# The relation-count product of a two-layer graph kernel: one float32 product against bfloat16 products on a table split in three

## Chip, cores, metric

One core of a Trainium2 chip. The metric is the device time of the kernel in microseconds, the median of repeated executions; all executions quoted here are fast (TensorE's granted clock 0.99 of full speed).

## The reference

128 graphs of 64 nodes with 768 features pass through two pre-norm layers. Only layer 0 matters here. `adj` holds 0 and 1, and serves both as the matrix and as the relation ids.

```python
h = jnp.maximum(_layernorm(x), 0.0)
ctx = jnp.matmul(adj, hs @ Wadj.T + badj) / deg_c[..., None]
ctx = ctx + jnp.matmul(radj, hs @ Wrev.T + brev) / rdeg_c[..., None]
ctx = ctx + hs @ Wself.T + bself
agg = jnp.einsum('bij,bijr->bir', adj, E[rels])
rel = agg @ Wr.T + br * deg[..., None]
ragg = jnp.einsum('bij,bijr->bir', radj, E[rr])       # rr: reversed ids + 40
rel = rel + ragg @ Wrr.T + brr * rdeg[..., None]
x = x + ctx + rel
```

## The kernel before

Two graphs make a tile of 128 rows, 64 tiles in all. The relation term is written as (count of each id in a row) times (id x E[id] W^T): 78 counts and 5 bias factors, one more product into the sums of layer 0. The program is unrolled, and the compiler of the kernel language orders each engine's instructions itself, by priority and by what it believes to be ready; every engine then runs its list strictly in that order. The stages are emitted as b(t), e(t-2), c(t), a(t+1), f(t-2), d(t-1).

```python
psb = tile_pool(name="psb", bufs=2, space=PSUM)       # products, two banks each
pss = tile_pool(name="pss", bufs=4, space=PSUM)       # transposes, one bank each
...
def stage_a(t):                                       # VectorE: counts of rows and columns
    H0[t] = norm_relu(X[t], "h0", 1)
    for d in range(2):
        eq = work.tile([P, NV, N], BF16, name="eq", bufs=1)
        nc.vector.tensor_tensor(eq, AB[c][...], vals, op=OP.is_equal)
        nc.vector.tensor_reduce(CNT[c][:, k, d*NV:(d+1)*NV], eq, AX.X, OP.add)

def stage_b(t):
    pt = pss.tile([P, 3, P], F32, name="ps")
    for d in range(2):
        nc.tensor.transpose(pt[:, d, :], ABD[c][:, k, d, :], ident)      # L252
    nc.tensor.transpose(pt[:NROW, 2, :], CNT[c][:, k, :], ident)         # L253
    r = R[t] = work.tile([P, 2, P], F32, name="r")
    nc.scalar.copy(r, pt[:, 0:2, :])                                     # L255
    CT_T[t] = work.tile([NROW, P], F32, name="cntT")
    nc.scalar.copy(CT_T[t], pt[:NROW, 2, :])                             # L257
    for kb in range(KB):
        ps = pss.tile([P, 3, P], F32, name="ps")
        nc.tensor.transpose(ps[:, 2, :], hb_, ident)                     # L262
        nc.tensor.matmul(ps[:, 0:2, :], hb_, r, start=True, stop=True)   # L263
        nc.scalar.copy(s1[:, kb], ps)

def stage_c(t):
    ... 36 float32 products of 384 columns                               # L275
    for hf in range(2):
        nc.tensor.matmul(pc[:, hf, :HALF], CT_T[t],
                         tab[:, hf*HALF:(hf+1)*HALF], start=False, stop=True)   # L280
    nc.vector.tensor_add(xv, pc[:, :, :HALF], xv)                        # L283, the residual add
    H1[t] = norm_relu(X[t], "h1", 3)
```

## Time and profile before

| | before |
|---|---|
| median time (three executions) | 3142.4 us (3140.8 to 3143.3) |
| TensorE busy, share of the chain | 98%, 95% |
| one tile in the steady state (L340 of one tile to the next, 2906.20 to 3050.08 us over three) | 47.96 us |
| first stage of tile 0 / of tile 1 starts | 37.0 us / 73.4 us |
| VectorE waits for TensorE ahead of tile 0's residual add | 18.5 us |

The chain of waits is nearly all TensorE, so the time is read as: start, plus 64 periods of TensorE's list, plus an end. The prediction shows the lines for the period.

### The profile page before, as it was taken

Reading aid. Unit: us, or ns where it says so; the run is one execution under the profiler, and the core shown is the slowest. Engines: PE = TensorE matmul, PEld = TensorE weight load, DVE = VectorE, ACT = ScalarE, POOL = GpSimd, SP = SyncE. Lnnn points to the kernel's source line nnn. Section 1 sums busy time; section 2 is a strip of 40 time slices with the busy share of each in tenths; the row PEclk is TensorE's granted clock in tenths of the full one; section 3 lists DMA queues with packets and bytes.
Section 4 is the critical chain, followed back from the end, with each engine's and each line's share of the span. In section 5 each row is a group of like instructions: output and inputs, shape, how many; then the busy total and the mean of one; then the engine's idle time right before and its main releaser. Section 6 shows DMA issues by size and latency. Waiting matters only on the chain.

```text
span 3139.9 us, 27406 instructions
## 1 busy us (share of the span) xinstructions
PE 3065.2 (98%) x10952; PEld 1908.4 (61%) x10952; DVE 1721.6 (55%) x2250; ACT 632.0 (20%) x1217; POOL 560.0 (18%) x556
## 2 busy tenths in 40 slices
PE   5999999999999999999999999999999999999997
PEld 3666666666666666666666666666666666666664
DVE  6356545565445565455654455654556544556344
ACT  1121121121121211211211212212112112122121
POOL 1112122121121121221211211212212112112121
PEclk8999999999999999999999999999999999999998
DMA  5000000000000000000000000000000000000000
GB/s 202 1 22 22 12 22 20 12 22 12 22 21 12 22 22 12 22 21 12 22 12 22 21 12 22 22 12 22 20 12 22 12 22 20 12 22 22 11 16 16
DMA packets 41065, 70.18 MB, mean 22 GB/s; under 512 B 19941, under 2 KB 20069, under 8 KB 40938
## 3 DMA queue, kind: packets, MB, share of 16 engines
q1 hardware_dynamic: 35840, 54.54, 5.4%
q10 hardware_dynamic: 5098, 13.89, 1.1%
q8 instruction: 87, 1.43, 0.2%
q14 instruction: 40, 0.33, 0.0%
HBM read 43.24 MB, written 25.17 MB: 22 GB/s over the span
## 4 chain that ended last, share of the span: by engine, by line
PE 95%; ACT 3%; DMA 1%; issue 1%; DVE 0%; ACTq 0%; POOL 0%; SPq 0%
PE pb L275 47%; PE pb L302 32%; PE ps L263 6%; PE pb L368 3%; PE pb L280 3%; PE ps L340 1%; ACT h1t L296 1%; ACT pT L364 1%; PE ps L363 1%; ACT r L255 1%; PE ps L262 1%; DMA wh<-in_w_cat_dram 0%; DMA xt<-in_x_dram 0%; PE ps L295 0%; ACTq L134 0%
## 5 line engine op out<-in xcount | busy, mean ns | idle before, releaser
L275 PE MATMUL pb<-w,s 128*128 128x384 f32 x4608 | 1496.6, 486 | 0.0
L275 PEld LDWEIGHTS pb<-w,s 128*128 128x128 f32 x4608 | 875.8, 190 | 609.9
L302 PE MATMUL pb<-wh,h1t 128*128 128x384 f32 x1536 | 512.5, 490 | 5.4 <-ACT h1t L296 0.6
L302 PE MATMUL pb<-wg,h1t 128*128 128x384 f32 x1536 | 505.8, 486 | 0.0
L283 DVE TENSOR_TENSOR xt<-pb,xt 128x768 f32<-128x768 f32 x64 | 61.3, 957 | 782.7 <-PE pb L280 782.6
L302 PEld LDWEIGHTS pb<-wg,h1t 128*128 128x128 f32 x1536 | 291.9, 190 | 203.4
L302 PEld LDWEIGHTS pb<-wh,h1t 128*128 128x128 f32 x1536 | 286.7, 190 | 207.0 <-ACT h1t L296 20.6
L243 DVE TENSOR_REDUCE cnt<-eq 128x39 f32<-128x2496 bf16 x128 | 352.4, 2753 | 3.2
L364 ACT COPY pT<-ps 128x384 f32<-128x384 f32 x128 | 55.2, 482 | 1294.6 <-PE ps L363 1294.5
L311 POOL MEMSET hs<- 128x6 f32 x64 | 7.3, 114 | 1377.5 <-PE pb L368 1377.5
L263 PE MATMUL ps<-r,h 128*128 128x256 f32 x768 | 209.5, 395 | 8.3
L241 DVE TENSOR_TENSOR eq<-ab,vals 128x2496 bf16<-128x2496 bf16 x128 | 186.6, 1458 | 3.6
L319 POOL TENSOR_TENSOR pr<-th,wsd 128x768 f32<-128x768 f32 x64 | 116.0, 1812 | 351.9 <-ACT th L309 351.9
L264 ACT COPY s<-ps 128x384 f32<-128x384 f32 x384 | 159.1, 497 | 46.1 <-PE ps L263 45.9
L342 DVE TENSOR_TENSOR a<-ps,sd 128x384 f32<-128x384 f32 x64 | 35.7, 557 | 213.6 <-PE ps L340 213.6
L263 PEld LDWEIGHTS ps<-r,h 128*128 128x128 f32 x768 | 128.0, 194 | 40.6 <-ACT r L255 23.0
L325 DVE TENSOR_TENSOR tg<-pb,hbb 128x768 f32<-128x768 f32 x64 | 61.3, 957 | 134.8 <-PE pb L302 134.8
L345 POOL MEMSET lm<- 128x384 f32 x64 | 26.7, 417 | 608.2 <-ACT pbd L353 608.2
L193 DVE BATCH_NORM_STATS2 st<-xt 128x6 f32<-128x384 f32 x256 | 127.2, 538 | 5.0 <-DMA xt<-in_x_dram 2.8
L199 POOL TENSOR_TENSOR rs<-ve,mhalf 128x1 f32<-128x1 f32 x128 | 107.7, 851 | 103.0 <-DVE ve L197 102.8
L377 DVE TENSOR_SCALAR e<-f 128x768 f32<-128x768 f32 x64 | 120.5, 1882 | 2.2
L202 ACT ACTIVATE h<-h,rs 128x768 f32<-128x768 f32 x128 | 113.3, 931 | 33.0 <-POOL rs L199 33.0
(70 smaller groups left out, 2300.2 us busy)
## 6 DMA issues: line engine op xcount, KB each, us to landing
xt<-in_x_dram SPq DMA_DIRECT2D x64, 384.0 KB, 3.5
out_dram<-f SPq DMA_DIRECT2D x64, 384.0 KB, 2.6
w<-in_wself_t_dram ACTq DMA_DIRECT2D x3, 768.0 KB, 8.2
w<-in_wadj_t_dram ACTq DMA_DIRECT2D x3, 768.0 KB, 11.2
w<-in_wrev_t_dram ACTq DMA_DIRECT2D x3, 768.0 KB, 13.8
wh<-in_w_cat_dram ACTq DMA_DIRECT2D x3, 768.0 KB, 15.0
wg<-in_hw_t_dram ACTq DMA_DIRECT2D x3, 768.0 KB, 15.4
ai<-in_adj_dram SPq DMA_DIRECT2D x32, 64.0 KB, 2.0
```

The costliest lines, as they stand in the source:

```text
L193: nc.vector.bn_stats(st[:, i, :], src[:, i * HALF : (i + 1) * HALF])
L199: nc.gpsimd.tensor_tensor(rs, ve, mhalf, op=OP.pow)
L202: nc.scalar.activation(h, h, AF.Copy, scale=rs)
L241: nc.vector.tensor_tensor(eq, AB[c][:, k, d, None, :].to_broadcast([P, NV, N]), vals, op=OP.is_equal)
L243: nc.vector.tensor_reduce(CNT[c][:, k, d * NV : (d + 1) * NV], eq, AX.X, OP.add)
L263: nc.tensor.matmul(ps[:, 0:2, :], hb_, r, start=True, stop=True)
L264: nc.scalar.copy(s1[:, kb], ps)
L275: nc.tensor.matmul(pc[:, hf, :HALF], S1T[t][:, kb, s, :], ws[s][:, kb, hf * HALF : (hf + 1) * HALF], start=(n == 0), stop=False)
L280: nc.tensor.matmul(pc[:, hf, :HALF], CT_T[t], tab[:, hf * HALF : (hf + 1) * HALF], start=False, stop=True)
L302: nc.tensor.matmul(p[:, hf, :HALF], h1t[:, kb, :], w[:, kb, hf * HALF : (hf + 1) * HALF], start=(kb == 0), stop=(kb == KB - 1))
L319: nc.gpsimd.tensor_mul(to, th, wsd[:, s, :])
L377: nc.vector.tensor_scalar(e, f, 0.0, None, op0=OP.min)
```

## The change

The counts are whole numbers up to 64, exact in bfloat16. The float32 table is split into three bfloat16 parts, whose sum is meant to be the table, and the parts are stacked along the contraction, so that one pass with float32 accumulation should give the float32 result. The counts have then to be repeated three times. 81 rows (the five bias rows are folded into three) times three are 243, more than 128: two parts of 126 and 117. The intent is to trade the four passes of a float32 product for two products of one pass each, 645 ns for 2 x 163 ns.

```diff
-    NROW = NCNT + 5
+    NROW = NCNT + 3
+    PARTS = ((0, P // 3), (P // 3, NROW))
...
-    tab = const.tile([NROW, D], F32, name="tab")
+    tabs = [const.tile([3 * (b - a), D], BF16, name=f"tab{a}") for a, b in PARTS]
...  # table: both parts, each row three times, by float32 products; then on VectorE
+        for i in range(3):
+            nc.vector.tensor_copy(q[:m], v[:m])
+            nc.vector.tensor_sub(v[:m], v[:m], q[:m])
+            nc.vector.scalar_tensor_tensor(u[:m], q[:m], part[:m, i : i + 1], u[:m],
+                                           op0=OP.mult, op1=OP.add)
+        nc.vector.tensor_copy(tab, u[:m])
...
-        cnt = CNT[c] = work.tile([P, CT, NROW], F32, name="cnt")
+        cnt = CNT[c] = work.tile([P, CT, NROW], BF16, name="cnt")
...
-        nc.tensor.transpose(pt[:NROW, 2, :], CNT[c][:, k, :], ident)
+        pn = pss.tile([P, 2, P], BF16, name="ps")
+        cn = CT_T[t] = work.tile([P, 2, P], BF16, name="cntT")
+        c3 = work.tile([P, NROW, 3], BF16, name="c3")
+        nc.gpsimd.tensor_copy(c3, CNT[c][:, k, :, None].to_broadcast([P, NROW, 3]))
+        for i, (a, b) in enumerate(PARTS):
+            nc.tensor.transpose(pn[: 3 * (b - a), i, :],
+                                c3[:, a:b, :].rearrange("p v c -> p (v c)"), identb)
+            nc.scalar.copy(cn[: 3 * (b - a), i, :], pn[: 3 * (b - a), i, :])
         r = R[t] = work.tile([P, 2, P], F32, name="r")
         nc.scalar.copy(r, pt[:, 0:2, :])
-        CT_T[t] = work.tile([NROW, P], F32, name="cntT")
-        nc.scalar.copy(CT_T[t], pt[:NROW, 2, :])
...
-            nc.tensor.matmul(pc[:, hf, :HALF], CT_T[t], tab[:, hf * HALF : (hf + 1) * HALF],
-                             start=False, stop=True)
+            for i, (a, b) in enumerate(PARTS):
+                nc.tensor.matmul(pc[:, hf, :HALF], CT_T[t][: 3 * (b - a), i, :],
+                                 tabs[i][:, hf * HALF : (hf + 1) * HALF],
+                                 start=False, stop=(i == 1))
```

More of the change, by code (lines that the diff above doesn't have):

```diff
@@ L74 @@
     NCNT = 2 * NV
-    NROW = NCNT + 5
+    NROW = NCNT + 3
+    PARTS = ((0, P // 3), (P // 3, NROW))
     W = DO + 1
-    assert GT == 2 and N == 64 and DO == P and H == KB and NROW <= P and NT % CT == 0
+    assert GT == 2 and N == 64 and DO == P and H == KB and 3 * (NROW - P // 3) <= P and NT % CT == 0
     xf = x.rearrange("g n d -> (g n) d")
@@ L129 @@
     nc.scalar.dma_start(wrt[:, 1, :], wrr_t)
+    bia = work.tile([5, D], F32, name="bia", tag="pr", bufs=1)
     for i, v in enumerate((br, brr, badj, brev, bself)):
-        nc.scalar.dma_start(tab[NCNT + i : NCNT + i + 1, :], row(v, 1))
+        nc.scalar.dma_start(bia[i : i + 1, :], row(v, 1))
     for w, src in ((ws[2], wself_t), (ws[0], wadj_t), (ws[1], wrev_t), (wh, w_cat), (wg, hw_t)):
@@ L145 @@
     make_identity(nc, ident)
+    identb = const.tile([P, P], BF16, name="identb")
+    nc.vector.tensor_copy(identb, ident)
     blk = const.tile([P, P], F32, name="blk")
@@ L173 @@
                    allow_small_or_imprecise_dtypes=True)
-    es = const.tile([P, 2, NCNT], F32, name="es")
+    es = const.tile([P, 2, NROW], F32, name="es")
     nc.vector.memset(es, 0.0)
@@ L178 @@
                              et[:, d * NB + 1 : (d + 1) * NB], ids)
-    pt = psb.tile([P, 2, 512], F32, name="pb")
-    for hf in range(2):
-        for d in range(2):
-            nc.tensor.matmul(pt[:NCNT, hf, :HALF], es[:, d, :],
-                             wrt[:, d, hf * HALF : (hf + 1) * HALF],
-                             start=(d == 0), stop=(d == 1))
-    nc.vector.tensor_copy(tab[:NCNT, :].rearrange("p (a b) -> p a b", a=2),
-                          pt[:NCNT, :, :HALF])
+    eb = const.tile([5, NROW], F32, name="eb")
@@ new lines @@
+    nc.gpsimd.memset(eb, 0.0)
+    nc.gpsimd.iota(eb[0:1, 0:NV], pattern=[[1, NV]], base=1, channel_multiplier=0,
+                   allow_small_or_imprecise_dtypes=True)
+    ebr = const.tile([1, NROW], F32, name="ebr")
+    nc.gpsimd.memset(ebr, 0.0)
+    nc.gpsimd.iota(ebr[0:1, NV:NCNT], pattern=[[1, NV]], base=1, channel_multiplier=0,
+                   allow_small_or_imprecise_dtypes=True)
+    nc.sync.dma_start(eb[1:2, :], ebr)
+    nc.sync.dma_start(eb[2:5, NCNT:NROW], ident[0:3, 0:3])
@@ new lines @@
+    part = const.tile([P, 3], F32, name="part")
+    for i in range(3):
+        nc.vector.tensor_reduce(
+            part[:, i : i + 1], ident[:, i:P:3],
+            AX.X, OP.add)
+    for (a, b), tab in zip(PARTS, tabs):
+        m = 3 * (b - a)
+        lhs = work.tile([P, 3, P], F32, name="lhs", tag="a", bufs=1)
+        for d in range(2):
+            nc.vector.tensor_copy(lhs[:, d, :m].rearrange("p (v c) -> p v c", c=3),
+                                  es[:, d, a:b, None].to_broadcast([P, b - a, 3]))
+        nc.vector.tensor_copy(lhs[:5, 2, :m].rearrange("p (v c) -> p v c", c=3),
+                              eb[:, a:b, None].to_broadcast([5, b - a, 3]))
+        pt = psb.tile([P, 2, 512], F32, name="pb")
+        for hf in range(2):
+            s = slice(hf * HALF, (hf + 1) * HALF)
+            for d in range(2):
+                nc.tensor.matmul(pt[:m, hf, :HALF], lhs[:, d, :m], wrt[:, d, s],
+                                 start=(d == 0), stop=False)
+            nc.tensor.matmul(pt[:m, hf, :HALF], lhs[:5, 2, :m], bia[:, s],
+                             start=False, stop=True)
+        v = work.tile([P, D], F32, name="tv", tag="e", bufs=1)
+        u = work.tile([P, D], F32, name="tu", tag="th", bufs=1)
+        q = work.tile([P, D], BF16, name="tq", tag="lm", bufs=1)
+        nc.vector.tensor_copy(v[:m].rearrange("p (a b) -> p a b", a=2), pt[:m, :, :HALF])
+        nc.gpsimd.memset(u, 0.0)
+        for i in range(3):
+            nc.vector.tensor_copy(q[:m], v[:m])
[3 more added lines that the diff above has]
+        nc.vector.tensor_copy(tab, u[:m])
@@ L215, in prep_adj @@
         nc.gpsimd.tensor_copy(AB[c], af)
-        cnt = CNT[c] = work.tile([P, CT, NROW], F32, name="cnt")
-        nc.vector.tensor_reduce(cnt[:, :, NCNT : NCNT + 2], af, AX.X, OP.add)
+        cnt = CNT[c] = work.tile([P, CT, NROW], BF16, name="cnt")
+        dg0 = small.tile([P, CT, 2], F32, name="dg0")
+        nc.vector.tensor_reduce(dg0, af, AX.X, OP.add)
         dc = small.tile([P, CT, 2], F32, name="dc")
-        nc.vector.tensor_scalar(dc, cnt[:, :, NCNT : NCNT + 2], 1.0, None, op0=OP.max)
+        nc.vector.tensor_scalar(dc, dg0, 1.0, None, op0=OP.max)
         rc = small.tile([P, CT, 2], F32, name="rc")
         nc.vector.reciprocal(rc, dc)
-        nc.vector.tensor_mul(cnt[:, :, NCNT + 2 : NCNT + 4], cnt[:, :, NCNT : NCNT + 2], rc)
-        nc.vector.memset(cnt[:, :, NCNT + 4 : NCNT + 5], 1.0)
+        nc.vector.tensor_scalar(cnt[:, :, NCNT : NCNT + 2], dg0, 1.0, None, op0=OP.min)
+        nc.vector.memset(cnt[:, :, NCNT + 2 : NCNT + 3], 1.0)
         ABD[c] = abds[c % 2]
@@ L242, in stage_a @@
                 eq, AB[c][:, k, d, None, :].to_broadcast([P, NV, N]), vals, op=OP.is_equal)
-            nc.vector.tensor_reduce(CNT[c][:, k, d * NV : (d + 1) * NV], eq, AX.X, OP.add)
+            with nc.allow_low_precision(reason="whole numbers up to 64"):
+                nc.vector.tensor_reduce(CNT[c][:, k, d * NV : (d + 1) * NV], eq, AX.X, OP.add)
     def stage_b(t):
```

## The prediction

> **What bounds the kernel now.** I read the page first: the busy shares, then the chain that ended last.
>
> ```profile
> span 3139.9 us, 27406 instructions
> PE 3065.2 (98%) x10952; PEld 1908.4 (61%) x10952; DVE 1721.6 (55%) x2250; ACT 632.0 (20%) x1217; POOL 560.0 (18%) x556
> ...
> PE 95%; ACT 3%; DMA 1%; issue 1%; DVE 0%; ACTq 0%; POOL 0%; SPq 0%
> ```
>
> TensorE is both 98% busy and 95% of the chain, so time that is taken off TensorE's stream is time taken off the span, and work on the other engines counts only where TensorE waits for it. The share of the touched product is in the groups by shape:
>
> ```profile
> L275 PE MATMUL pb<-w,s 128*128 128x384 f32 x4608 | 1496.6, 486 | 0.0
> L280 PE MATMUL pb<-tab,cntT 83*128 83x384 f32 x256 | 93.1, 485 | 0.0
> L253 PE MATMUL ps<-ident,cnt 128*83 128x128 f32 x64 | 17.7, 276 | 5.4 <-DVE cnt L243 5.4
> L257 ACT COPY cntT<-ps 83x128 f32<-83x128 f32 x64 | 16.9, 264 | 0.0
> L215 POOL CAST ab<-af 128x256 bf16<-128x256 f32 x32 | 12.7, 396 | 30.0 <-DVE af L213 30.0
> ```
>
> L280 is the count product: 256 records for 64 tiles x 2 halves, so one float32 matmul is two records. The mean of 485 ns is not its price, because the recorded windows overlap (4608 x 486 ns would be 2239 us where the union is 1497). For the price I read the chain in order of time through one tile of the steady state; it gives start-to-start times.
>
> ```profile
> 1564.07 23.22 PE pb L275 x72
> 1587.29 1.29 PE pb L280 x4
> ...
> 1591.88 15.75 PE pb L302 x48
> 1607.63 0.12 PE ps L253
> 1607.75 0.02 issue
> 1607.77 0.38 ACT r L255
> 1608.15 0.04 issue
> 1608.20 1.56 PE ps L263 x6
> ```
>
> 23.22 us / 72 = 322.5 ns per record, so 645 ns per float32 product of 384 columns, and 1.29 us per tile for L280's two products. Over 64 tiles that is 82.6 us, 2.6% of the span: the most that this part could give back. The last five lines show a second thing: after the gate's product TensorE transposes the counts (L253), ScalarE then copies r, and only then can L263 begin. The timeline of TensorE one tile earlier says how much of this is idle:
>
> ```profile
> 1559.50 0.27 PE L253 MATMUL ps<-ident,cnt 128*83 128x128 f32 x1
> 1559.61 0.49 PE L262 MATMUL ps<-ident,h 128*128 128x128 f32 x3
> 1560.24 1.56 PE L263 MATMUL ps<-r,h 128*128 128x256 f32 x6
> ...
> 1591.42 0.38 PE L252 MATMUL ps<-ident,abd 128*128 128x128 f32 x2
> 1591.88 1.56 PE L302 MATMUL pb<-wh,h1t 128*128 128x384 f32 x4
> ```
>
> A float32 transpose starts every 0.11 us here (1559.50 to 1559.61), so three L262 end their slots at 1559.94, and L263 starts at 1560.24: 0.30 us idle per tile. The matrices that r comes from (L252) were transposed early, in the hole ahead of L302; r is late only because its PSUM tile also takes the count transpose. The period is 48.0 us; adding up the slots (72, 4 and 48 records at 0.3225 us, 22 transposes at 0.11, 12 L263 at 0.216, 12 L368 at 0.11, L340 0.645) gives 46.9 us, so all idling is only some 1.1 us per tile.
>
> **What the Trainium skill says.** "Perfetto Trace Analysis", section Tensor Engine Instruction: the profiler's start of a matmul is real, its end is computed. The trace agrees (486 ns windows every 322.5 ns), so I use starts only. "FP8 and Floating Point Precision", section TensorE Precision Notes: true float32 takes four passes through the array. "TensorE: Matmul & The Clock Gate", section Back-to-back issue gap: N / 2.4 + 2.5 ns at full clock. Four passes of 384 columns at 2.4 GHz are 640 ns; the trace has 645 in two records, so it agrees with both. No instruction of this trace is a bfloat16 matmul, so the price of the new product is an estimate from that page: 384 / 2.4 + 2.5 = 162.5 ns, and 55.8 ns for a transpose with 128 columns. "PSUM — Partial Sum Buffer", section on bank collisions: two engines must not touch one bank and quadrant at once, so accesses are to be ordered by bank, not by address. The kernel before never reads one part of a transposed tile before writing the next, so its trace cannot show the effect; the changed one does exactly that.
>
> **The change, part by part.**
>
> *Removed.* Four L280 records per tile (1.29 us), one float32 count transpose (0.11 us), one ScalarE copy of 83x128 (0.26 us, not on the path), and the tie of r to the count transpose (up to 0.30 us).
>
> *Added on TensorE.* Stacking three parts makes 243 rows, more than 128, hence two parts of 126 and 117 rows. That is 2 parts x 2 halves = 4 bfloat16 products of one pass each: 4 x 162.5 = 0.65 us. The threefold contraction costs two instructions for one, not three times. Their weight loads are at most 0.14 us (the shortest float32 load recorded) and hide behind 0.16 us of matmul. Two bfloat16 transposes: 2 x 0.056 = 0.11 us. Net on TensorE's slots: 1.29 + 0.11 - 0.65 - 0.11 = 0.64 us per tile, 41 us over 64 tiles.
>
> *Moved.* r now has a PSUM tile of its own, complete with L252. Those transposes run some 15 us before the stage that uses r, and ScalarE (20% busy) can copy it meanwhile. I expect most of the 0.30 us idle to go: 0.3 x 64 = 19 us.
>
> *Added elsewhere.* GpSimd writes every count three times: 243 bfloat16 elements, near the 256-element cast of 0.40 us, so 64 x 0.4 = 26 us on an engine at 18%. The counts are made by VectorE well ahead (TensorE waited for them twice, both at the start), so this copy should be early too. ScalarE gets two copies of 128 columns for one, +0.26 us per tile. The minimum in place of the product of degrees costs VectorE nothing new.
>
> *Added wait.* Both count transposes write one PSUM bank, and ScalarE copies the first part between them: the second must wait for transpose latency plus copy, 0.27 + 0.26 + handoffs = about 0.6 us. TensorE has three L262 (0.33 us) and L263 pairs (0.43 us each) to put in between, if the instruction order does so. I charge 0.1 us per tile, 6 us.
>
> *Start.* The split table takes VectorE about 2 parts x 11 passes over 768 columns at 0.6 to 0.96 us, some 20 us, and TensorE 24 float32 records instead of 8. The first stage now begins at 36.97 us, held by the queue of DMA issues on ScalarE (until 34.6 us), and the table is read only at 66 us; VectorE fills this time with counts of tiles that are not urgent. Most of it is hidden; I charge 3 us because the order of the first counts and copies may slip.
>
> Sum: 41 + 19 - 6 - 3 = 51 us, or 3142 - 51 = 3091 us, 1.6% faster.
>
> **The rivals.**
>
> *The handoff between the transposes replaces r's wait.* For it: the write-read-write of one bank, and ScalarE having the gate's tanh (0.85 us) in the same stretch, in strict order. Against it: other work lies ready for TensorE. If the whole 0.6 us shows each tile, 38 us are lost: 41 + 19 - 38 - 3 = 19 us gained, 3123 us.
>
> *The gap fillers go further.* With counts ready far ahead, the transposes can slide into the holes before L368 and L302 (about 0.24 us idle each), so they cost nothing, and r's wait goes altogether: (0.645 + 0.30 + 0.11 + 0.1) x 64 = 74 us, 3068 us. For it: L252 sits in such a hole already. Against it: that hole is 0.24 us and L253 was not put there before.
>
> *Only the passes count.* r is copied late for some other reason, as ScalarE's order puts it behind the count copies: 41 - 6 - 3 = 32 us, 3110 us.
>
> *Slower.* The GpSimd copy lands on the path (it queues behind the two 1.81 us products with the tanh), or the table's set-up delays the first stage by 20 us. Either costs up to 60 us; GpSimd's idle stretch of 20 us in every period speaks against the first, the DMA issues until 34.6 us against the second.
>
> **Range and chances.** The 41 us rest on pass counts that the trace confirms; the order of instructions decides the rest, some 20 us either way. I centre between the sum and the second rival's ceiling at 3090 us and hold 3067 to 3115 eight times in ten. Two per cent is 62.8 us, 0.98 us per tile: it needs the idling to go as well as the passes, 22%. Slower by 2% needs a new stall of 1.6 us per tile: 2%.
>
> **What would show it.** In the profile after: four records of L280's successor in 0.65 us of the chain (1.2 or more would say that bfloat16 does not save the passes); no ScalarE copy of r in the chain between L302 and L263; a period near 47.15 us; second count transposes after a ScalarE wait, with TensorE idle below 0.1 us; GpSimd at about 19%; the first product of layer 0 still near 43 us. A first stage beyond 45 us, or GpSimd in the chain, would make the prediction wrong.

## More of the kernel before

CNT, the buffer of the counts, holds a chunk of two tiles and exists twice.

VectorE's timeline around the first residual add and TensorE's at the second tile (start, duration, engine, line, operation; in brackets the idle time before it and what ended it):

```profile
47.38 1.46 DVE L241 TENSOR_TENSOR eq<-ab,vals 128x2496 bf16<-128x2496 bf16 x1
67.36 0.96 DVE L283 TENSOR_TENSOR xt<-pb,xt 128x768 f32<-128x768 f32 x1 [18.52 <-PE pb L280]
```

```profile
73.40 0.48 PE L262 MATMUL ps<-ident,h 128*128 128x128 f32 x1 [5.75 <-ACT h L202]
```

VectorE has 18.5 us of slack there; the second tile's first stage needs a normalisation that stands behind this add in VectorE's list.

## The result, and the profile after

The changed kernel takes 3094.7 us (3092.9 to 3095.7) beside 3142.1 us of the kernel before (four executions): 47.4 us less, ratio 0.985, 95% interval 0.9836 to 0.9864. The gain is clear of the noise, but at the 2% line the verdict is "same". A ratio here is the mean time of one kernel's fast runs over that of the other's fast runs of the same rounds, so it is not quite the ratio of the medians that are quoted.

The line numbers shift: L241 and L243 (the comparison and the reduction that make the counts) are L286 and L289 now, L252 is L298, L253 is L304, L255 is L308, L262/L263 are L313/L314, L275 is L326, L280 is L332, L283 is L336, L302 (heads and gate) is L355, and L340 (the logits' product) is L393. The page of the changed kernel shows the same bound:

```profile
span 3092.7 us, 27801 instructions
PE 3023.1 (98%) x11032; PEld 1886.3 (61%) x11032; DVE 1736.7 (56%) x2281; ACT 643.6 (21%) x1281; POOL 589.8 (19%) x626
```

The chain in order of time, one tile of the steady state (start, duration, what):

```profile
1575.31 15.75 PE pb L355 x48
1591.05 0.06 PE ps L304
1591.11 0.12 PE ps L313
1591.22 0.43 PE ps L314 x2
1591.66 0.06 PE ps L304
...
1594.44 0.65 PE ps L393 x2
1595.08 23.22 PE pb L326 x72
1618.30 0.66 PE pb L332 x4
```

Three things are to be seen. The count products take 0.66 us where they took 1.29. ScalarE's copy of r is gone from between the gate's product and L314: r was copied at 1575.52 us, 15 us early. And the second count transpose stands behind one L313 and one L314, so that ScalarE's copy between the two transposes costs TensorE nothing. From the end of L355 to the start of the logits' product (L393) 3.39 us pass; in the kernel before it was 3.76 us (1607.63 to 1611.39). The period is 46.945 us (L393 at 2909.18 and 3003.07, two tiles), 1.015 us less than before. From the second tile's first stage to the end of the program the profiled execution takes 3003.0 us (3092.7 less 89.7) where it took 3066.5 us (3139.9 less 73.4): 63.5 us less, which is 1.015 us for some 62.5 tiles. That is 16 us more than the whole gain, so 16 us were lost before that, at the start. VectorE's timeline around the first residual add, and TensorE's at the second tile, in the changed kernel:

```profile
66.17 1.46 DVE L286 TENSOR_TENSOR eq<-ab,vals 128x2496 bf16<-128x2496 bf16 x1
67.67 2.75 DVE L289 TENSOR_REDUCE cnt<-eq 128x39 bf16<-128x2496 bf16 x1
...
80.51 2.75 DVE L289 TENSOR_REDUCE cnt<-eq 128x39 bf16<-128x2496 bf16 x1
83.18 0.95 DVE L336 TENSOR_TENSOR xt<-pb,xt 128x768 f32<-128x768 f32 x1
```

```profile
66.59 0.82 PE L332 MATMUL pb<-tab,cntT 126*128 126x384 bf16 x4
...
89.66 0.47 PE L313 MATMUL ps<-ident,h 128*128 128x128 f32 x1 [21.18 <-ACT h L246]
```

TensorE finishes the first tile's products at about 67.4 us, as before, but VectorE comes to the add only at 83.2 us, with no idle before it: it is busy with counts of tiles that nobody needs yet. The second tile starts at 89.7 us instead of 73.4: 16.3 us later. VectorE's list ahead of this add grew by two things: by the table (2 x 11 passes and the small copies, some 16 us) and by counts (from 8 to 12 reductions and from 9 to 12 comparisons, 15.6 us). The theory that I tested: GpSimd's threefold copy reads the counts early and so frees their buffer early, which lets the list's maker put the next chunk's counts into VectorE's hole ahead of the add. (The expectations below price them at 17 us, four pairs of 4.2 us; one of the four comparisons stood there before the change too.) The account closes: in the kernel before, VectorE's list ahead of the add ended at 48.84 us (47.38 + 1.46), now it ends at 83.18 us. These 34.3 us are 15.6 us of counts, 2.4 us more waiting of VectorE, and some 16 us of table; less the hole of 18.5 us they leave 15.8 us, by which the add is late (83.18 against 67.36 us). By these sizes either load alone would fit; e1 shows it for the table.

### The profile page after: what moved, and what is told of

Read it like the earlier page. It is cut to its first block, busy times and chain, and to the rows that moved or that the text cites. A ratio compares the mean times of both kernels' runs of the same rounds, so it can differ in the third digit from the quotient of the medians.

```text
span 3092.7 us, 27801 instructions
## 1 busy us (share of the span) xinstructions
PE 3023.1 (98%) x11032; PEld 1886.3 (61%) x11032; DVE 1736.7 (56%) x2281; ACT 643.6 (21%) x1281; POOL 589.8 (19%) x626
## 4 chain that ended last, share of the span: by engine, by line
PE 94%; DVE 2%; ACT 2%; issue 1%; DMA 0%; POOL 0%; ACTq 0%; SPq 0%; DVEq 0%; POOLq 0%
PE pb L326 47%; PE pb L355 33%; PE ps L314 5%; PE pb L421 3%; PE ps L313 1%; PE pb L332 1%; PE ps L393 1%; ACT h1t L349 1%; ACT pT L417 1%; DVE cnt L289 1%; PE ps L416 1%; DVE eq L286 0%; PE ps L348 0%; PE pb L216 0%; PE ps L304 0%
## 5 line engine op out<-in xcount | busy, mean ns | idle before, releaser
L326 PE MATMUL pb<-w,s 128*128 128x384 f32 x4608 | 1496.6, 486 | 0.0
L326 PEld LDWEIGHTS pb<-w,s 128*128 128x128 f32 x4608 | 877.2, 190 | 608.4
L355 PE MATMUL pb<-wh,h1t 128*128 128x384 f32 x1536 | 512.5, 491 | 5.3 <-ACT h1t L349 0.6
L355 PE MATMUL pb<-wg,h1t 128*128 128x384 f32 x1536 | 505.9, 486 | 0.0
L336 DVE TENSOR_TENSOR xt<-pb,xt 128x768 f32<-128x768 f32 x64 | 61.3, 958 | 743.4 <-PE pb L332 743.4
L355 PEld LDWEIGHTS pb<-wg,h1t 128*128 128x128 f32 x1536 | 292.4, 190 | 202.9
L355 PEld LDWEIGHTS pb<-wh,h1t 128*128 128x128 f32 x1536 | 287.1, 190 | 206.6 <-ACT h1t L349 20.6
L289 DVE TENSOR_REDUCE cnt<-eq 128x39 bf16<-128x2496 bf16 x128 | 352.3, 2752 | 3.1
L314 PE MATMUL ps<-r,h 128*128 128x256 f32 x768 | 219.8, 386 | 0.0
L286 DVE TENSOR_TENSOR eq<-ab,vals 128x2496 bf16<-128x2496 bf16 x128 | 186.7, 1459 | 3.4
L313 PE MATMUL ps<-ident,h 128*128 128x128 f32 x384 | 107.1, 279 | 25.8 <-ACT h L246 25.8
L314 PEld LDWEIGHTS ps<-r,h 128*128 128x128 f32 x768 | 119.2, 196 | 18.1 <-issue 1.4
L306 ACT COPY cntT<-ps 126x128 bf16<-126x128 bf16 (+1 forms) x128 | 34.3, 268 | 429.7 <-PE ps L304 429.7
L243 POOL TENSOR_TENSOR rs<-ve,mhalf 128x1 f32<-128x1 f32 x128 | 107.8, 852 | 76.9 <-DVE ve L241 76.7
```

The source lines that it names most:

```text
L243: nc.gpsimd.tensor_tensor(rs, ve, mhalf, op=OP.pow)
L286: nc.vector.tensor_tensor(eq, AB[c][:, k, d, None, :].to_broadcast([P, NV, N]), vals, op=OP.is_equal)
L289: nc.vector.tensor_reduce(CNT[c][:, k, d * NV : (d + 1) * NV], eq, AX.X, OP.add)
L326: nc.tensor.matmul(pc[:, hf, :HALF], S1T[t][:, kb, s, :], ws[s][:, kb, hf * HALF : (hf + 1) * HALF], start=(n == 0), stop=False)
L355: nc.tensor.matmul(p[:, hf, :HALF], h1t[:, kb, :], w[:, kb, hf * HALF : (hf + 1) * HALF], start=(kb == 0), stop=(kb == KB - 1))
```

## The experiments

"Correct" below means that the output passed the check. The kernel before took 3141.3 us beside e1 to e4 and 3142.3 us beside e5 to e8. Unless the text says otherwise the edit is on the changed kernel.

### e1: hold the counts until TensorE has read them

```diff
-        cnt = CNT[c] = work.tile([P, CT, NROW], BF16, name="cnt")
+        cnt = CNT[c] = work.tile([P, CT, NROW, 3], BF16, name="cnt")
...  # counts, minima and the one are written to [..., 0]
-        c3 = work.tile([P, NROW, 3], BF16, name="c3")
-        nc.gpsimd.tensor_copy(c3, CNT[c][:, k, :, None].to_broadcast([P, NROW, 3]))
+        c3 = CNT[c][:, k]
+        nc.gpsimd.tensor_copy(c3[:, :, 1:3], c3[:, :, 0:1].to_broadcast([P, NROW, 2]))
```

> The changed kernel, but the threefold copies of the counts lie in the counts' own buffer, so that the buffer comes free only when TensorE has transposed them, as in the kernel before. Theory (two loads meet in VectorE's order before the first layer-0 residual add: the table's 19 us and the counts of tiles that the early copy lets in, 17 us; the slack is 18.5 us): the add of tile 0 starts at about 67.3 us instead of 83.2, the second tile's first stage near 73 us instead of 89.7, period unchanged at 46.95 us, time 3095 - 16 = 3079 us (3077 to 3082). Rival (the table alone delays the start): 3095 us within 2. Rival (the early copy is needed in the steady state): period above 46.95 us and a time above 3082 us.

Correct, 3078.4 us (3077.1 to 3078.6), ratio 0.9799 (0.9784 to 0.9814). VectorE's and TensorE's timelines of e1:

```profile
67.36 0.96 DVE L336 TENSOR_TENSOR xt<-pb,xt 128x768 f32<-128x768 f32 x1 [2.26 <-PE pb L332]
```

```profile
73.40 0.48 PE L313 MATMUL ps<-ident,h 128*128 128x128 f32 x1 [5.01 <-ACT h L246]
```

The add waits for TensorE again, the second tile starts at 73.40 us, exactly as in the kernel before, and the period stays 46.95 us. The 16.3 us come back as 16.3 us of time. The table's work is still all there, so the table alone does not delay the start; it leaves 2.26 us of the slack. This version beats both kernels; against the kernel before the interval reaches over the 2% line, so that verdict is unclear.

### e5: the table's split cut to one round

```diff
         for i in range(3):
+            if i > 0:
+                continue
             nc.vector.tensor_copy(q[:m], v[:m])
```

> The changed kernel with the table's split stopped after its first round: the two lower parts of the table stay zero, so the product has bfloat16's precision only; VectorE loses 12 passes over 768 columns, some 9.3 us in the changed kernel's trace, and nothing else; all twelve counts still stand ahead of the residual add in VectorE's order. Theory (the start's delay is the length of VectorE's queue beyond the slack, whatever it is made of): the add of tile 0 at 83.2 - 9.3 = 73.9 us, the second tile's first stage near 80.4 us, time 3094.7 - 9.3 = 3085.4 us (3084 to 3087). Rival (only the early counts matter, the table hides): 3094.7 us within 2; also if VectorE's copies wait for something else, such as TensorE's table products.

Correct, 3087.3 us (3086.3 to 3087.7), ratio 0.9825, 0.3 us above the expected range and far from the rival. The add (L338 here) starts at 74.47 us, still without a wait, and the second tile's first stage at 80.95 us, 8.7 us earlier than in the changed kernel, where 9.3 were expected; some of the removed time turned into waits of VectorE for the table's products. The median fell by 7.4 us, the profiled span by 8.2. VectorE's add in e5:

```profile
74.47 0.95 DVE L338 TENSOR_TENSOR xt<-pb,xt 128x768 f32<-128x768 f32 x1
```

So the length of VectorE's list counts: with the counts in place, less table brings the add forward nearly one to one. With e1 this shows that each of the two loads adds to the delay, and that the table needs the counts to do harm. The reverse, the counts without any table, was not run. An estimate: the ten passes of table that are left in e5 take 7.2 us in its trace, and the add is still 7.1 us late, so the counts alone would just about fit. A by-product: the run still passed as correct, so this check cannot tell the exact split from its first part.

### e2: the table's split on GpSimd

```diff
-            nc.vector.tensor_copy(q[:m], v[:m])
-            nc.vector.tensor_sub(v[:m], v[:m], q[:m])
-            nc.vector.scalar_tensor_tensor(u[:m], q[:m], part[:m, i : i + 1], u[:m],
-                                           op0=OP.mult, op1=OP.add)
-        nc.vector.tensor_copy(tab, u[:m])
+            nc.gpsimd.tensor_copy(q[:m], v[:m])
+            nc.gpsimd.tensor_sub(v[:m], v[:m], q[:m])
+            nc.gpsimd.tensor_scalar(q[:m], q[:m], part[:m, i : i + 1], None, op0=OP.mult)
+            nc.gpsimd.tensor_add(u[:m], u[:m], q[:m])
+        nc.gpsimd.tensor_copy(tab, u[:m])
```

> The changed kernel with the splitting of the table (14 passes over the 768 columns, 15.5 us of VectorE) on GpSimd; nothing else moves in the orders of the engines. Theory (both loads together exceed the slack of 18.5 us): VectorE's queue ahead of the residual add ends near 83.2 - 15.5 = 67.7 us, the second tile's first stage starts near 74 us, time about 3079 us (3077 to 3083). Rival (counts alone delay the start, the table is hidden): 3095 us within 2. If GpSimd's slower passes hold up the table itself beyond 66 us, the count product of tile 0 waits and the time lies between 3083 and 3095.

Correct, 3090.6 us (3089.6 to 3091.8), a miss: 4 us gained where 16 were expected. (The time lies in the last band of the expectation, but not for the reason given there: the table came late, and yet it is VectorE that holds the add. The edit also moves 20 passes and not 14.) VectorE's timeline of e2, while GpSimd works on the table:

```profile
54.79 2.83 DVE L286 TENSOR_TENSOR eq<-ab,vals 128x2496 bf16<-128x2496 bf16 x1
57.65 2.75 DVE L289 TENSOR_REDUCE cnt<-eq 128x39 bf16<-128x2496 bf16 x1
60.44 2.28 DVE L286 TENSOR_TENSOR eq<-ab,vals 128x2496 bf16<-128x2496 bf16 x1
...
78.70 0.95 DVE L336 TENSOR_TENSOR xt<-pb,xt 128x768 f32<-128x768 f32 x1
```

The comparisons take up to 2.83 us instead of 1.46 us (3.2 us more in all), while the reductions between them keep 2.75 us. The Trainium skill ("Advanced Engine Details and Errata", section GPSIMD Details) says that GpSimd and VectorE share a read and a write interface and that VectorE instructions with two SBUF inputs are among those that conflict. The trace agrees: the comparisons read two tiles in SBUF, the reductions one. VectorE also waits 6.5 us for GpSimd, since the second part's copy out of PSUM reuses a buffer. The add comes at 78.7 us. The work was moved, but a good part of its cost stayed with VectorE. The second part of the table came at 70.1 us, 3.8 us late for TensorE. As a test of the two loads e2 says little; e5 does it cleanly.

### e3: the kernel before, with the counts' transpose in a tile of its own

```diff
-        nc.tensor.transpose(pt[:NROW, 2, :], CNT[c][:, k, :], ident)
+        pn = pss.tile([P, P], F32, name="ps")
+        nc.tensor.transpose(pn[:NROW, :], CNT[c][:, k, :], ident)
...
-        nc.scalar.copy(CT_T[t], pt[:NROW, 2, :])
+        nc.scalar.copy(CT_T[t], pn[:NROW, :])
```

> The kernel before, float32 product and all, with only the transposed counts moved to a PSUM tile of their own, so that ScalarE can copy r early. Theory (r's wait is 0.30 to 0.37 us of every tile and belongs to the shared tile alone): period 47.96 - 0.3 to 0.37 = 47.6 to 47.66 us, no ScalarE copy of r in the chain, time 3142 - 19 to 24 = 3118 to 3123 us. Rival (the wait went because of the bfloat16 transposes and their order): 3142 us within 3. The start may also move by some us, since the order of the first copies changes.

Correct, 3117.9 us (3116.5 to 3118.8), ratio 0.9925 (0.991 to 0.994): 23.3 us from one PSUM tile, without any bfloat16. The chain of e3:

```profile
1626.24 15.75 PE pb L303 x48
1641.99 0.11 PE ps L254
1642.10 0.11 PE ps L263
1642.21 0.43 PE ps L264 x2
...
1645.36 0.65 PE ps L341 x2
```

ScalarE's copy of r is out of the chain. From L303's end to the logits' product 3.37 us pass, against 3.76: 0.39 us. The period is 47.57 us (L341 at 2929.77 and 2977.34), 0.39 us below 47.96. This is more than the 0.30 us that I had read off the timeline as idle: with r early, each L263/L264 pair follows its transpose at once, and the later small stalls of that stage go as well.

### e6: r tied to the counts again, in the changed kernel

```diff
-        pn = pss.tile([P, 2, P], BF16, name="ps")
+        pn = pt[:, 2, :].bitcast(BF16).rearrange("p (a b) -> p a b", a=2)
```

> The changed kernel with the bfloat16 count transposes written into the last third of r's own PSUM tile, as the kernel before had it; same products. Theory (what e3 gave is taken back, and the write-read-write of one bank now shows as well): the copy of r is back in the chain between the gate's product and the first (A h) product; at least 0.37 us per tile, and by the chain transpose 0.27 + copy 0.26 + transpose 0.27 + copies of counts and r 0.27 + 0.37 less the three transposes in between 0.33 us up to 1.0 us per tile: period 47.3 to 47.95 us, time 3118 to 3159 us. Rival (with bfloat16 transposes the tie costs nothing): 3095 us within 3.

Correct, 3159.7 us (3158.9 to 3160.3), ratio 1.0056: slower than the kernel before (the late start is in it too), and 0.7 us beyond the upper end of what I expected. The chain of e6:

```profile
1624.05 0.06 PE ps L304
1624.11 0.33 PE ps L313 x3
...
1624.46 0.23 PE ps L304
...
1624.71 0.27 ACT cntT L306
1624.98 0.28 ACT r L308
...
1625.31 1.56 PE ps L314 x6
```

The period is 48.01 us (2924.98 to 2972.99), 1.07 us above the changed kernel's. All links of the expected path are there: three transposes fill 0.33 us, then the second count transpose, its copy, r's copy, L314. The rival of the prediction, "the handoff between the transposes replaces r's wait", is thus real; it fails to appear in the changed kernel because r has its own bank, the one line in which e6 differs. The tie would have cost more than the bfloat16 products save.

### e4: the kernel before without its count products

```diff
-                                     start=(n == 0), stop=False)
+                                     start=(n == 0), stop=(n == 3 * KB - 1))
...
-        for hf in range(2):
-            nc.tensor.matmul(pc[:, hf, :HALF], CT_T[t], tab[...], start=False, stop=True)
```

> The kernel before without the two count products of each tile; wrong on purpose, it measures what the product cost. Theory (its whole start-to-start time of 1.29 us lies on the path): period 46.67 us, time 3142 - 82.6 = 3059 us (3056 to 3063). Rival (part of it hides waits of other engines that would show without it, such as the exponentials' transposes behind it): above 3065 us.

3058.5 us (3057.6 to 3061.0): 82.7 us less, against 82.6 expected. Its output is wrong, which doesn't matter for the time. The period is 46.67 us. The float32 product cost its start-to-start time to within the noise; nothing was hidden beside it.

### e7: each bfloat16 product twice

```diff
+                for j in range(2):
-                nc.tensor.matmul(..., start=False, stop=(i == 1))
+                    nc.tensor.matmul(..., start=False, stop=(i == 1 and j == 1))
```

> The changed kernel with each of the four bfloat16 count products issued twice (wrong on purpose: the relation term counts double); orders otherwise equal. Theory (a bfloat16 product of 384 columns costs 0.163 us of path, its weight load hidden): 8 records in 1.3 us, period 46.95 + 0.65 = 47.6 us, time 3094.7 + 0.65 x 64 = 3136 us (3134 to 3139). Rival (loads of weights show when products repeat, or part of the cost hides): outside this by more than 5 us.

3134.3 us (3134.1 to 3135.2): 39.6 us more than the changed kernel. Its output is wrong, which doesn't matter for the time. The chain has

```profile
1590.46 1.31 PE pb L333 x8
```

in place of 0.66 us for four, and the period is 47.59 us, 0.65 us up: 0.163 us per product. The missing 2 us lie partly at the start, where the second tile began at 88.6 us instead of 89.7.

### e8: e1 with the weights issued by SyncE

```diff
-            nc.scalar.dma_start(w[:, k : k + 2, :], ...)
+            nc.sync.dma_start(w[:, k : k + 2, :], ...)
...  # likewise the rows bb, hbb, wsd; the two small loads into eb go to ScalarE
```

> The kernel of e1 with the 15 weight loads and the four small rows issued from SyncE's queue in place of ScalarE's, so that ScalarE is free for the first normalisation at about 12 us and not at 35 us. Not a test of the change but a try at the rest of the start. Expected: the first stage begins before 20 us instead of 37.6; the first product then runs as the weights land, and ends near 50 us instead of 66.5, period unchanged 46.95 us; time 3078.4 - 10 to 17 = 3061 to 3068 us. Rival (the start is bound by the weights' 35 us of transfer or by the second activations' chain anyway): 3078 us within 3. If the later loads of x, queued behind the weights, come late, it is slower than e1.

Correct, 3070.8 us (3070.3 to 3072.2), ratio 0.9774 (0.9759 to 0.9789): 7.6 us better than e1 and beyond 2% against the kernel before, but a miss: 10 to 17 us were expected, and the first stage begins at 23.3 us, not before 20. The chain at the start:

```profile
29.81 1.48 PE pb L216 x4
...
33.35 23.22 PE pb L326 x72
56.57 0.67 PE pb L332 x4
57.27 0.96 DVE xt L336
58.23 2.66 DVE cnt L289
```

The first tile's products begin at 33.35 instead of 43.3 us. They are now held by the float32 products of the table (L216), which stand between the transposes in TensorE's list, and the second tile by a count reduction (2.66 us) behind the residual add. So about 10 us are gained and 2.7 given back. This is beside the change; it shows that the start still has a few us in it.

## Why the prediction was right

The predicted 3090 us and the measured 3094.7 us agree, and the steady state changed as the prediction said: four records in 0.66 us of the chain, no copy of r in it, GpSimd at 19%. But the terms of the sum did not all come out. The steady state gave some 10 us more than the sum has, and the start cost 13 us more; that these two errors cancelled is luck.

| step of the prediction | predicted | measured |
|---|---|---|
| passes and transposes, 0.64 us per tile | -41 us | -40 us (1.29 to 0.66 us per tile, e4 and e7) |
| r's idle, 0.30 us per tile | -19 us | -24 us (0.37 to 0.39 us per tile, e3) |
| the transposes' handoff, 0.1 us per tile | +6 us | 0 (no idle in the chain; 1.07 us per tile when r is tied, e6) |
| the start | +3 us | +16.3 us (73.4 to 89.7 us; e1 takes it away) |
| sum | -51 us | -48 us (measured time: -47.4 us) |

**The passes** were right to a few per cent: both the ceiling of 82.6 us (e4) and the bfloat16 price of 0.1625 us per product (0.163 us in e7). The Trainium skill ("TensorE: Matmul & The Clock Gate", section Back-to-back issue gap) gives the formula behind this price for isolated matmuls only, with other figures for streams with weight loads; the prediction left that out, and for this shape e7 sides with the formula.

**r's idle** was the right mechanism, sized somewhat low. I counted the one gap ahead of L263 and not the small stalls behind it. (The prediction's sum of slots counts 22 transposes where a tile has 21; no term rests on it.)

**The handoff** was charged and did not occur. Its mechanism exists, but the instruction order put other work between the two transposes, as the prediction said it might.

**The start** is the step that failed. The prediction said "Most of it is hidden; I charge 3 us because the order of the first counts and copies may slip", and judged the start by TensorE's and ScalarE's side: the first stage at 37 us, the table read at 66 us. Both held (37.4 us, 66.6 us). What I did not do was to add up VectorE's list up to the first residual add, where 18.5 us were free. The table alone does hide there (e1, with 2.26 us to spare), but I missed that the early copy would release the counts' buffer and so let 15.6 us of future counts in front of the same add. The prediction even welcomed the early copy ("so this copy should be early too"). The rival "Slower" came nearest: it has the table's set-up delay the start, but through the first stage and not through VectorE's list.

**The 2% line** was given 22%. The steady state delivered what that needed, 1.0 us per tile against the stated 0.98; the start took it away. e1, which keeps the first and repairs the second, lies just on the line.

**What stays open.** That the early release of the counts' buffer is what moves the counts forward is shown by e1's edit and by the lists; why the maker of the lists put them ahead of an add that was ready 16 us earlier was not looked into. The early release without the table, say a third counts' buffer in the kernel before, was not run. Some 1 to 2 us between the sum of the terms and the measured times in e5, e7 and e8 are not traced.

## What to carry to other kernels

Where one engine bounds the kernel, split a change into slots of that engine's list, price each by start-to-start times, and look for waits tied to a shared buffer: here a PSUM tile of its own gave 23 us by itself, more than half of what the cheaper products gave. Then add up, for every other engine, what stands in its list ahead of the first thing that the bound engine waits for; slack at the start is a budget, and work of set-up and work let in by a buffer that comes free earlier draw on it together. An engine relieved by moving work to a neighbour may keep much of the cost as waits and contention (e2), so time the neighbour's effect as well.

## What the Trainium skill lacked or had wrong

- No page says that a buffer released earlier can make a kernel slower, because an engine of strict order gets later tiles' work ahead of urgent work. Here, together with the table's work: 16.3 us at the start (89.7 against 73.4 us), taken back by e1.
- No page has the price of a write-read-write chain between TensorE and ScalarE in one PSUM bank. Here: 1.07 us per tile when r's copy waits behind it too (e6), of which r's wait alone is 0.39 us in the kernel before (e3); nothing when r has its own bank.
- "TensorE: Matmul & The Clock Gate", section Part 4, gives some 275 ns for a 128x128 bfloat16 transpose in a kernel. The trace's recorded window is 221 ns, but in a stream the next instruction starts after 0.06 us (0.11 us for float32), so the slot is what to count.
